# A diffusion-transformer block: two spare PSUM banks in the last attention unit, the next row's weights issued by ScalarE, and six weight pieces made earlier

## The chip, the cores and the metric

The kernel runs on one core of a Trainium2 chip. The metric is device time in microseconds (us) for one launch, lower is better. In the profile PE is TensorE (matmuls), PEld its weight loads, DVE is VectorE, ACT is ScalarE, POOL is GpSimd and SP is SyncE, which here issues most of the DMA transfers ("SPq" is its queue). "L192" is line 192 of the kernel; the matmuls go through a helper, so nearly all of them carry this line and are told apart by the names of their tiles.

## The reference

One transformer block with adaptive layer norm, in float32, for `x` of shape (2, 2048, 512) and a condition of shape (2, 512). There are 16 heads of 32 channels, the attention is causal, and the hidden layer is 2048 wide.

```python
mod = silu(condition) @ Wada + bada
sh_a, sc_a, gt_a, sh_m, sc_m, gt_m = jnp.split(mod, 6, axis=1)
xm = layernorm(x, g1, be1) * (1.0 + sc_a[:, None, :]) + sh_a[:, None, :]
q, k, v = (xm @ Wqkv)            # 16 heads of 32
attn = softmax(where(causal, q @ k.T * 32**-0.5, -inf))
x = x + gt_a[:, None, :] * ((attn @ v) @ Wproj + bproj)
xm = layernorm(x, g2, be2) * (1.0 + sc_m[:, None, :]) + sh_m[:, None, :]
x = x + gt_m[:, None, :] * (gelu(xm @ W1 + b1) @ W2 + b2)
```

## The kernel before

The two batch rows are worked one after the other, and then both go through the hidden layer. In order of time: QKV projection of row 0, attention of row 0, output projection of row 0, QKV projection of row 1, attention of row 1, output projection of row 1, hidden layer. TensorE's matmuls, and the calls wrapped in `act(...)`, are kept in the order of the program; everything else is ordered by a scheduler when the kernel is built. Each engine works its own list in order, and so does each DMA queue: an entry that waits holds up all that stand behind it.

**QKV projection** (`Qkv.run`, `Qkv.group`). Four groups `g` of 512 tokens, each with 12 products `n` (eight for queries and keys, four for values). The weights `wqkv`, 3 MB, are loaded in three pieces by `load_w`. After every product, `also(g, n)` may put in other work. In row 0 it makes the modulation out of `Wada`, whose halves pass one after the other through a tile of the pool `wada`. The `x` tiles of the next group are loaded, normalised and transposed between the products, and scores of the first attention units are put between the matmuls.

**Attention** (`attention_phase`). A unit is four heads (index `c`) and 512 queries (block `i`); there are 16, and the last has `i = 3`. A unit is worked in steps, one for each block of 128 keys: 15 steps in the last unit. In a step, `scores_t` makes the transposed scores of four heads in four PSUM banks `st`: four "fold" matmuls write the negative row maxima (`st<-fold,sel`), four more add the scores (`st<-qst,kst`), and ScalarE takes the exponential of each bank into a tile `e` (L558). Two steps later the products with the values (`o<-e,vv`) follow, and now and then the row sums (`sm<-ee,ones`). The row maxima come from scores made ahead in the two banks of the pool `ps_s` (tag `s`); in the last unit none are left to make. PSUM's eight banks are four `st` (`bufs=HC`, and HC is 4), two `s`, one `o` and one `sm`.

Each unit's sums are inverted and widened to all channels in DRAM (`wide_d`). In the last unit, `prepare(n)` readies the projection at step `n`: it loads the projection weights (`wproj`), old outputs (`at_s`) and `x` tiles into memory of keys no longer used, multiplies the weights by the gate (`ps_gate`, one matmul `ps_rows` into an `s` bank), and loads two blocks of widened inverses (`rb_s`) into old query tiles.

**Output projection** (`project_phase`). Four blocks `k` of 512 tokens in four tiles of 128. For each tile GpSimd adds the bias to the residual input (`xt`, L938), TensorE makes four products (`ps_o`), VectorE adds them to `xt` (L945), takes statistics (L204), the result goes to DRAM (`x1d`, L947), and VectorE scales one quarter of the next block's `at` by its inverses (L951). TensorE can therefore begin block `k + 1` only when VectorE has come so far with block `k`. In blocks 1 to 3 the `xt` tiles are loaded at this time, into four buffers. `between(n)` is called after each tile `n`; in row 0 it starts, at `n = 4`, the load of row 1's weights:

```python
        def between(n):
            if n == 4:
                qkv.load_w()
```

**Weight pieces** (`Quarters`). The hidden layer multiplies with a scheme of seven products in place of eight, whose weights are sums and differences of quarters. GpSimd makes them, 16 pieces in all (`FC`), each from four loads of 128 KB, five additions of 128x256 and a store of 896 KB to DRAM (`w1d`, `w2d`). All 16 are made during row 1's QKV projection; two of the four loads go to a tile of their own, `w1r`.

Of the kernel before, what the change touches and what calls it, by code (L numbers as in the profile page):

```python
# [8 lines left out]
F32 = mybir.dt.float32  # L9
# [3 lines left out]
ALU = mybir.AluOpType  # L13
# [4 lines left out]
P = 128  # L18
# [3 lines left out]
QB = 512  # L22
# [5 lines left out]
def dit_block_kernel(  # L28
# [35 lines left out]
    nc = tc.nc  # L64
    B, T, D = x.shape
    HID = W1.shape[1]
    C = D // P
    FC = HID // P
    NT = T // P
    HC = P // HD  # L70
# [3 lines left out]
    NG = T // MT  # L74
# [8 lines left out]
    def pool(name, bufs=1, **kw):  # L83
        return tc.tile_pool(name=name, bufs=bufs, reuse_waits="tile", **kw)
# [25 lines left out]
        op=ALU.add,  # L110
# [3 lines left out]
    for n in range(2):  # L114

        f = bp.tile([P, QB + P], F32R, tag=f"fold{n}", name=f"fold{n}")
# [7 lines left out]
    for r in (0, HD):  # L124
# [19 lines left out]
    bgate = bp.tile([P, D], F32, tag="bgate", name="bgate")  # L144
# [20 lines left out]
    wide_d = [  # L165
        [dram.tile([P, C, QB], F32, tag=f"wide{b}{i}", name=f"wide{b}{i}") for i in range(NQ)]
        for b in range(B)
    ]
# [25 lines left out]
    def act(ins):  # L194

        return tc.keep_in_program_order(ins)
# [14 lines left out]
    def rows_of(psum, r, b, tag):  # L211

        ps = psum.tile([P, D], F32, tag=tag, name="ps_rows")
        g = slice(r * HD, (r + 1) * HD)
        mm(ps, pick[g, b, :], modr[g, :], start=True, stop=True)
        return ps
# [43 lines left out]
    units = []  # L260
# [4 lines left out]
    last_order = [i for _, i in units[-NQ:]]  # L265
# [6 lines left out]
    ps_sp = ps_s_cm.__enter__()  # L272

    class Row:


        def __init__(self, b):
            self.b = b
            self.vv = bp.tile([P, NT, D], F32, tag="vv", name="vv")
            self.kst, self.qst, self.pools = {}, {}, {0: bp}  # L280
            self.at = 0
            self.todo = [
                (u, h, t, kb)
                for u, (_, i) in enumerate(units)
                for h in range(HC)
                for t in range(TQ)
                for kb in range(i + 1)
            ]
            self.mx = None
            self.spent = 0  # L290
            self.rows_made = 0
# [106 lines left out]
        def prepare(self, n):  # L398

            if n == 3:  # L400
                self.prefetch()
            elif n == 5:
                self.ps_gate = rows_of(ps_sp, 0, self.b, "s")
                act(nc.vector.tensor_tensor(bgate, bgate, self.ps_gate, ALU.mult))
            elif n == 7:
                self.rb_s = [self.old_queries() for _ in range(2)]
                for k in range(2):
                    nc.sync.dma_start(self.rb_s[k], wide_d[self.b][last_order[k]])
            if 5 <= n < 5 + C:
                w = self.wproj[:, n - 5, :]  # L410
                act(nc.vector.tensor_tensor(w, w, self.ps_gate, ALU.mult))
            elif 11 <= n < 11 + C:
                d, r = self.at_s[0][:, n - 11, :], self.rb_s[0][:, n - 11, :]
                act(nc.vector.tensor_tensor(d, d, r, ALU.mult))

# [97 lines left out]
    def attention_phase(row):  # L513
        b, vv, kst, qst = row.b, row.vv, row.kst, row.qst
        with pool(f"att{b}") as ap, pool(
            f"ps_st{b}", bufs=HC, space=PSUM
        ) as ps_stp, pool(f"ps_o{b}", space=PSUM) as ps_op:
            row.pools[1] = ap

            def scores_t(u, step, n):  # L520

                def st_bank():
                    return ps_stp.tile([P, QB], F32, tag="st", name="st")  # L530

                c, i = units[u]
                tiles = steps_of[u][step]
                q0 = tiles[0][1]
                w = sum(QB - q for _, q in tiles)
                sts, es = [], []
                row.score(max(0, n - 5))
                n = min(n, 5)
                for h in range(HC):
                    g = slice(h * HD, (h + 1) * HD)  # L540
                    st = st_bank()
                    mm(
                        st[:, :w], sel[g, :], fold[u % 2][g, q0 : q0 + w],
                        start=True, stop=False,
                    )
                    sts.append(st)
                for h in range(HC):
                    at = 0
                    for j, q in tiles:
                        mm(  # L550
                            sts[h][:, at : at + QB - q],
                            kst[c][:, h, j * P : (j + 1) * P],
                            qst[u][:, h, q:],
                            start=False, stop=at + QB - q == w,
                        )
                        at += QB - q
                    e = ap.tile([P, QB], F32, tag="e", name="e", bufs=E_BUFS)
                    act(nc.scalar.activation(e[:, :w], sts[h][:, :w], AF.Exp))  # L558
                    if tiles[0][0] >= i * TQ:

                        d = e.rearrange("p (t k) -> p t k", k=P)[:, 0 : TQ : TQ - 1, :]
                        d = d[:, : len(tiles), :]
                        act(
                            nc.gpsimd.affine_select(  # L564
                                d, d, pattern=[[0, len(tiles)], [1, P]],
                                compare_op=ALU.is_ge, fill=0.0,
                                base=0, channel_multiplier=-1,
                            )
                        )
                    es.append(e)  # L570
                    if h >= HC - n:
                        row.score(1, st_bank if h == 2 else None)
                row.score(n - HC)
                return es
# [55 lines left out]
            for u, (c, i) in enumerate(units):  # L630
                for n, tiles in enumerate(steps_of[u]):
                    w = sum(QB - q for _, q in tiles)
# [12 lines left out]
            for u, (c, i) in enumerate(units):  # L645
# [5 lines left out]
                for n_step, tiles in enumerate(steps_of[u]):  # L651
                    last = n_step == steps - 1
                    if n_step == 0:
# [4 lines left out]
                    n = row.count(  # L658
                        due(u, starts[u] + n_step) - QB // 2, u + AHEAD
                    )  # L660
# [70 lines left out]
    class Qkv:  # L731
# [12 lines left out]
                xts.append(xt)  # L744
            self.xts[g] = xts

        def load_w(self):
            w_v = Wqkv.rearrange("(c p) f -> p c f", p=P)
            for f in range(0, 3 * D, D):
                nc.sync.dma_start(self.w[:, :, f : f + D], w_v[:, :, f : f + D])  # L750

        def norm(self, g, j):

# [90 lines left out]
    w1_v = W1.rearrange("(c p) f -> p c f", p=P)  # L844
    w2_v = W2.rearrange("(c p) f -> p c f", p=P)

    class Quarters:


# [1 line left out]

        def __init__(self, cp):
            self.cp, self.at = cp, 0
            self.to = []

        def quarters(self, f):
# [13 lines left out]
                for k, n in ((0, f), (1, g), (0, g), (1, f))  # L872
            ]

        def step(self):

            while self.to:
                dst, w = self.to.pop()
                nc.gpsimd.dma_start(dst, w)
            f, self.at = self.at, self.at + 1  # L880
            if f >= FC:
                return
            w = self.cp.tile([P, 7, C // 2, P], F32, tag="w7", name="w7", bufs=2)
            raw = self.cp.tile([P, 2, C // 2, P], F32, tag="w1r", name="w1r", bufs=2)
            for dst, src in zip((w[:, 2], w[:, 1], raw[:, 0], raw[:, 1]), self.quarters(f)):
                nc.gpsimd.dma_start(dst, src)
            for n, x, y, op in (
                (0, w[:, 2], w[:, 1], ALU.add),
                (3, w[:, 2], raw[:, 0], ALU.add),
                (4, raw[:, 1], w[:, 1], ALU.add),  # L890
                (5, raw[:, 1], w[:, 2], ALU.subtract),
                (6, w[:, 1], raw[:, 0], ALU.subtract),
            ):
                nc.gpsimd.tensor_tensor(w[:, n], x, y, op)
            if f < FC // 2:
                self.to.append((w1d[f], w))
            else:
                self.to.append(
                    (w2d[:, f - FC // 2], w.rearrange("p n c d -> p n (c d)"))
                )  # L900
# [58 lines left out]
    with pool("wada") as wp, pool("qkv0") as qp, pool(  # L959
# [32 lines left out]
        qkv = Qkv(row, qp, ps_mm)  # L992
        qkv.load_x(0)
        load_wada(0, 1)
        qkv.load_w()

        ps_c = ps_mm.tile([P, n_rows], F32, tag="mm", name="ps_c")
        transpose(ps_c, rows)
# [46 lines left out]

        def also(g, n):

            if g == 0 and n == 2:
                load_wada(2, 5)
            elif g == 1 and n == 3:  # L1050
                modulation(2)
                load_wada(3, 4)
            elif g == 2 and n == 3:
                modulation(3)
                scale_shift(a2, c2, r_g2, r_be2, 3, 4)

        with pool("hl0") as hp:
            qkv.run(hp, also)

    attention_phase(row)  # L1060


    first, row = row, Row(1)
    with pool("qkv1") as qp, pool("ps_qkv1", bufs=6, space=PSUM) as ps_mm:
        qkv = Qkv(row, qp, ps_mm)
        qkv.xts[0] = first.next_s

        def between(n):
            if n == 4:
                qkv.load_w()  # L1070
            if n in (5, 8):
                qkv.norm(0, n // 8)()

        project_phase(first, ps_mm, between)

        def also(g, n):
            if n % 3 == 1:
                quarters.step()

        with pool("hl1") as hp:  # L1080
            quarters = Quarters(hp)
            qkv.run(hp, also)
            quarters.step()

    attention_phase(row)
    ps_s_cm.__exit__(None, None, None)
# [350 lines left out]
```

## Time and profile before

| what | value |
|---|---|
| median of 3 runs | 2528.28 us (2524.02 to 2534.17) |
| the profiled execution: its own time, its span | 2531.33 us, 2529.6 us |
| PE busy | 2464.2 us, 97% of the span |
| PEld, DVE, ACT, POOL busy | 46%, 53%, 35%, 39% |
| granted TensorE clock, mean | 0.990 |
| DMA | 285.71 MB, mean 113 GB/s |
| QKV projection of row 0 | about 21 to 223 us |
| last attention unit of row 0, of row 1 | 753.9 to 805.5, 1604.5 to 1656.2 us |
| output projection of row 0, of row 1 | 805.5 to 874.6, 1656.2 to 1718.2 us |
| QKV projection of row 1 | 874.6 to 1074 us |
| hidden layer | 1718.2 us to the end |

A line of a timeline has the start, the time it took, the engine, the line, the operation, its output and inputs with their shapes, the number of instructions that were merged, and in brackets the idle time before it and what ended that. A line of stretches has, for each engine, busy time and number of instructions, then the granted clock, the DMA engines' busy share and GB/s. A matmul's end is modelled, so a matmul that waits inside a group of merged ones is drawn longer, and not as idle time.

### The profile page before, as it was taken

The numbers are of one execution on the slowest core, as the hardware profiler recorded it, in microseconds if no ns is written. First come the engines' busy times: TensorE is split into PE (matmuls) and PEld (weight loads), VectorE is DVE, ScalarE is ACT, GpSimd is POOL, SyncE is SP. The second block draws the span as 40 slices with busy tenths as digits, with TensorE's granted clock in tenths as the row PEclk, the third lists the DMA queues.
The fourth block names the chain that finished last, engine by engine and source line by source line (L and its number), as shares of the span: only waits on it lengthen the run. The fifth ranks groups of instructions, "written<-read, shape, count | busy, mean of one in ns | idle before, by whom it ended". The sixth has DMA issues, their size and how long they took to land.

```text
span 2529.6 us, 30921 instructions
## 1 busy us (share of the span) xinstructions
PE 2464.2 (97%) x10977; PEld 1174.0 (46%) x10977; DVE 1347.6 (53%) x2818; ACT 895.0 (35%) x1667; POOL 981.4 (39%) x1158
## 2 busy tenths in 40 slices
PE   7999999999999899999999999999999999999998
PEld 3445445454444344554444444444444444444443
DVE  3455657666556535656675756565353353344424
ACT  2213555555544011155545454613312312311310
POOL 0001776766761476168667775231101201200200
PEclk9999999999999999999999999999999999999999
DMA  6636123041332699540414113163223233322422
GB/s 223 207 123 155 39 59 77 22 109 43 96 114 91 212 302 295 172 102 22 109 43 103 32 47 137 52 213 125 85 94 127 90 100 106 110 91 73 139 84 96
DMA packets 133445, 285.71 MB, mean 113 GB/s; under 512 B 13301, under 2 KB 42525, under 8 KB 128426
## 3 DMA queue, kind: packets, MB, share of 16 engines
q1 hardware_dynamic: 127810, 260.61, 34.6%
q0 software_dynamic: 5376, 23.07, 2.6%
q8 instruction: 86, 1.41, 0.2%
q14 instruction: 69, 0.57, 0.1%
q10 hardware_dynamic: 104, 0.05, 0.0%
HBM read 209.76 MB, written 81.79 MB: 115 GB/s over the span
## 4 chain that ended last, share of the span: by engine, by line
PE 60%; DVE 2%; DMA 2%; SPq 1%; issue 1%; ACT 0%; POOL 0%; DVEq 0%; ACTq 0%; POOLq 0%
PE ps_y L192 15%; PE ps_h L192 15%; PE st L192 9%; PE o L192 5%; PE s L192 4%; PE ps_qk L192 4%; PE sm L192 2%; PE ps_o L192 2%; PE ps_v L192 2%; SPq L336 1%; DMA k<-hl 1%; PE ps_xt L200 1%; DVE junk L434 1%; DMA r<-sum 1%; DVE mx L439 0%
## 5 line engine op out<-in xcount | busy, mean ns | idle before, releaser
L558 ACT ACTIVATE e<-st 128x512 f32<-128x512 f32 (+1 forms) x1152 | 575.0, 576 | 516.4 <-PE st L192 467.3
L439 DVE TENSOR_REDUCE mx<-s 128x1 f32<-128x512 f32 x616 | 413.7, 687 | 274.5 <-PE s L192 273.3
L584 POOL TENSOR_TENSOR ee<-e 128x512 f32<-128x512 f32 x336 | 421.3, 1290 | 246.0 <-ACT e L558 245.5
L192 PE MATMUL s<-kst,qst 128*128 128x512 f32 (+3 forms) x1058 | 453.3, 447 | 18.7 <-DVE mx L434 9.2
L192 PE MATMUL st<-qst,kst 128*128 128x512 f32 (+3 forms) x1280 | 437.0, 391 | 0.0
L192 PE MATMUL o<-e,vv 128*32 128x512 f32 (+3 forms) x2560 | 295.6, 543 | 0.0
L192 PE MATMUL ps_h<-sx,w 128*128 128x512 f32 x640 | 286.7, 592 | 0.0
L564 POOL TENSOR_SCALAR_AFFINE_SELECT e<-e 128x128 f32<-128x128 f32 (+1 forms) x384 | 123.6, 340 | 416.8 <-ACT e L558 410.1
L434 DVE CUSTOM_DVE_ANT_0 junk<-s,causal 128x384 bf16<-128x384 f32 (+3 forms) x442 | 211.1, 478 | 135.6 <-PE s L192 126.9
L1208 POOL TENSOR_TENSOR c<-c 128x512 f32<-128x512 f32 x32 | 40.8, 1274 | 619.9 <-DVE c L1170 619.9
L192 PE MATMUL ps_y<-sh,w 128*128 128x512 f32 x640 | 277.9, 594 | 0.0
L192 PEld LDWEIGHTS st<-qst,kst 128*128 128x128 f32 x1280 | 229.5, 191 | 87.7 <-issue 63.1
L192 PEld LDWEIGHTS s<-kst,qst 128*128 128x128 f32 x1058 | 198.8, 189 | 144.2 <-issue 47.9
L192 PE MATMUL ps_qk<-xmT,wqkv 128*128 128x512 f32 x512 | 242.0, 601 | 2.2 <-DVE xmT L248 2.2
L1170 DVE TENSOR_TENSOR h<-c,ps_h 128x512 f32<-128x512 f32 x128 | 88.0, 688 | 232.5 <-PE ps_h L192 232.4
L584 POOL TENSOR_TENSOR ee<-ee 128x512 f32<-128x512 f32 x168 | 211.0, 1286 | 0.0
L192 PEld LDWEIGHTS ps_h<-sx,w 128*128 128x128 f32 x640 | 121.1, 190 | 150.2 <-issue 149.2
L192 PEld LDWEIGHTS ps_y<-sh,w 128*128 128x128 f32 x640 | 121.3, 191 | 148.6 <-issue 147.1
L192 PE MATMUL st<-fold,sel 32*128 32x512 f32 (+1 forms) x1152 | 163.6, 484 | 2.4 <-DVE mhl L454 1.1
L1194 ACT ACTIVATE h<-h,cols 128x512 f32<-128x512 f32 x128 | 92.4, 722 | 182.0 <-DVE h L1170 182.0
L192 PEld LDWEIGHTS st<-fold,sel 32*128 32x128 f32 x1152 | 65.5, 183 | 187.8 <-ACT e L558 136.5
L192 PEld LDWEIGHTS ps_qk<-xmT,wqkv 128*128 128x128 f32 x512 | 95.4, 193 | 98.8 <-issue 91.5
(126 smaller groups left out, 2362.3 us busy)
## 6 DMA issues: line engine op xcount, KB each, us to landing
qst<-q SPq DMA_DIRECT2D x128, 256.0 KB
w<-w1d SPq DMA_DIRECT2D x34, 896.0 KB
w<-w2d SPq DMA_DIRECT2D x28, 1024.0 KB
kst<-k SPq DMA_DIRECT2D x24, 1024.0 KB
q<-hl SPq DMA_DIRECT2D x32, 512.0 KB
k<-hl SPq DMA_DIRECT2D x32, 512.0 KB
kst<-k SPq DMA_DIRECT2D x32, 256.0 KB
o<-ot SPq DMA_DIRECT2D x32, 256.0 KB
```

Source lines behind the costliest of these rows:

```text
L192: return tc.keep_in_program_order(nc.tensor.matmul(*args, **kw))
L200: return tc.keep_in_program_order(nc.tensor.transpose(dst, src, ident[:n, :n]))
L336: nc.sync.dma_start(dst, inv_d[self.b][u].unsqueeze(1).to_broadcast([HC, HD, QB]),)
L434: nc.vector.tensor_tensor_reduce(junk[:, :w], s[:, :w], causal[:, QB - w :], 1.0, MASKED, ALU.add, ALU.max, m,)
L439: nc.vector.tensor_reduce(m, s[:, :w], axis=AX.X, op=ALU.max)
L558: act(nc.scalar.activation(e[:, :w], sts[h][:, :w], AF.Exp))
L564: nc.gpsimd.affine_select(d, d, pattern=[[0, len(tiles)], [1, P]], compare_op=ALU.is_ge, fill=0.0, base=0, channel_multiplier=-1,)
L584: act(engine.tensor_tensor(dst, x, y, ALU.add))
L1170: nc.vector.tensor_tensor(dst, x, y, op)
L1194: nc.scalar.activation(d, d, AF.Gelu, bias=col(r_b1 + chunk, 1))
L1208: nc.gpsimd.tensor_tensor(c1_, c1_, c2_, ALU.subtract)
```

## The change

Four edits.

- In the last unit `st_bank` takes some of its tiles from the two `s` banks: a counter is raised for each tile, and the tile goes to `s` where the counter modulo 6 is over `HC` (4).
- `prepare` no longer holds the gate in an `s` bank for four steps: it copies it at step 5 into the first quarter of `rb_s[1]`, scales the weights from there in steps 6 to 9 (before: 5 to 8), and loads `rb_s[0]` at step 5 and `rb_s[1]` at step 10 (before: both at 7).
- `load_w` takes the queue to issue on. In row 0's output projection it is called at `n == 2` on ScalarE's queue (before: at 4, on SyncE's).
- The first six of the sixteen weight pieces are made in the last group of row 0's QKV projection, at even `n`, two at a time in the memory of the `wada` tile; the other ten in row 1's, where a step comes every fourth product in place of every third. The two extra loads of a piece go to places of the piece itself, which are overwritten by the additions; `w1r` is gone.

TensorE's list of instructions stays as it was. ScalarE's list has the three `wqkv` loads behind the last unit's copy of `sums`.

```diff
--- before.py
+++ after.py
@@ -400,16 +400,18 @@
             if n == 3:
                 self.prefetch()
             elif n == 5:
-                self.ps_gate = rows_of(ps_sp, 0, self.b, "s")
-                act(nc.vector.tensor_tensor(bgate, bgate, self.ps_gate, ALU.mult))
-            elif n == 7:
+                ps = rows_of(ps_sp, 0, self.b, "s")
                 self.rb_s = [self.old_queries() for _ in range(2)]
-                for k in range(2):
-                    nc.sync.dma_start(self.rb_s[k], wide_d[self.b][last_order[k]])
-            if 5 <= n < 5 + C:
-                w = self.wproj[:, n - 5, :]
-                act(nc.vector.tensor_tensor(w, w, self.ps_gate, ALU.mult))
-            elif 11 <= n < 11 + C:
+                self.gate = self.rb_s[1][:, 0, :]
+                act(nc.vector.tensor_copy(self.gate, ps))
+                act(nc.vector.tensor_tensor(bgate, bgate, self.gate, ALU.mult))
+                nc.sync.dma_start(self.rb_s[0], wide_d[self.b][last_order[0]])
+            if 6 <= n < 6 + C:
+                w = self.wproj[:, n - 6, :]
+                act(nc.vector.tensor_tensor(w, w, self.gate, ALU.mult))
+            if n == 10:
+                nc.sync.dma_start(self.rb_s[1], wide_d[self.b][last_order[1]])
+            if 11 <= n < 11 + C:
                 d, r = self.at_s[0][:, n - 11, :], self.rb_s[0][:, n - 11, :]
                 act(nc.vector.tensor_tensor(d, d, r, ALU.mult))
 
@@ -517,6 +519,8 @@
         ) as ps_stp, pool(f"ps_o{b}", space=PSUM) as ps_op:
             row.pools[1] = ap
 
+            n_bank = [0]
+
             def scores_t(u, step, n):
 
 
@@ -527,6 +531,10 @@
 
 
                 def st_bank():
+
+                    n_bank[0] += u == len(units) - 1
+                    if n_bank[0] % 6 > HC:
+                        return ps_sp.tile([P, QB], F32, tag="s", name="st")
                     return ps_stp.tile([P, QB], F32, tag="st", name="st")
 
                 c, i = units[u]
@@ -744,10 +752,10 @@
                 xts.append(xt)
             self.xts[g] = xts
 
-        def load_w(self):
+        def load_w(self, queue):
             w_v = Wqkv.rearrange("(c p) f -> p c f", p=P)
             for f in range(0, 3 * D, D):
-                nc.sync.dma_start(self.w[:, :, f : f + D], w_v[:, :, f : f + D])
+                queue.dma_start(self.w[:, :, f : f + D], w_v[:, :, f : f + D])
 
         def norm(self, g, j):
 
@@ -844,6 +852,8 @@
     w1_v = W1.rearrange("(c p) f -> p c f", p=P)
     w2_v = W2.rearrange("(c p) f -> p c f", p=P)
 
+    piece = 7 * C // 2 * P
+
     class Quarters:
 
 
@@ -851,8 +861,8 @@
 
 
 
-        def __init__(self, cp):
-            self.cp, self.at = cp, 0
+        def __init__(self):
+            self.rooms, self.more_rooms, self.at = [], None, 0
             self.to = []
 
         def quarters(self, f):
@@ -872,26 +882,30 @@
                 for k, n in ((0, f), (1, g), (0, g), (1, f))
             ]
 
-        def step(self):
-
+        def store(self):
             while self.to:
                 dst, w = self.to.pop()
                 nc.gpsimd.dma_start(dst, w)
+
+        def step(self):
+
+            self.store()
             f, self.at = self.at, self.at + 1
             if f >= FC:
                 return
-            w = self.cp.tile([P, 7, C // 2, P], F32, tag="w7", name="w7", bufs=2)
-            raw = self.cp.tile([P, 2, C // 2, P], F32, tag="w1r", name="w1r", bufs=2)
-            for dst, src in zip((w[:, 2], w[:, 1], raw[:, 0], raw[:, 1]), self.quarters(f)):
-                nc.gpsimd.dma_start(dst, src)
+            if not self.rooms:
+                self.rooms = self.more_rooms()
+            w = self.rooms.pop(0).rearrange("p (n c d) -> p n c d", n=7, d=P)
+            for n, src in zip((2, 1, 6, 5), self.quarters(f)):
+                nc.gpsimd.dma_start(w[:, n], src)
             for n, x, y, op in (
-                (0, w[:, 2], w[:, 1], ALU.add),
-                (3, w[:, 2], raw[:, 0], ALU.add),
-                (4, raw[:, 1], w[:, 1], ALU.add),
-                (5, raw[:, 1], w[:, 2], ALU.subtract),
-                (6, w[:, 1], raw[:, 0], ALU.subtract),
+                (0, 2, 1, ALU.add),
+                (3, 2, 6, ALU.add),
+                (4, 5, 1, ALU.add),
+                (5, 5, 2, ALU.subtract),
+                (6, 1, 6, ALU.subtract),
             ):
-                nc.gpsimd.tensor_tensor(w[:, n], x, y, op)
+                nc.gpsimd.tensor_tensor(w[:, n], w[:, x], w[:, y], op)
             if f < FC // 2:
                 self.to.append((w1d[f], w))
             else:
@@ -992,7 +1006,7 @@
         qkv = Qkv(row, qp, ps_mm)
         qkv.load_x(0)
         load_wada(0, 1)
-        qkv.load_w()
+        qkv.load_w(nc.sync)
 
         ps_c = ps_mm.tile([P, n_rows], F32, tag="mm", name="ps_c")
         transpose(ps_c, rows)
@@ -1045,6 +1059,8 @@
 
         def also(g, n):
 
+            if g == NG - 1 and n % 2 == 0:
+                quarters.step()
             if g == 0 and n == 2:
                 load_wada(2, 5)
             elif g == 1 and n == 3:
@@ -1054,8 +1070,17 @@
                 modulation(3)
                 scale_shift(a2, c2, r_g2, r_be2, 3, 4)
 
+        quarters = Quarters()
         with pool("hl0") as hp:
+
+            def rooms():
+
+                w = wp.tile([P, 2 * C * D], F32, tag="wada", name="w7")
+                return [w[:, k * piece : (k + 1) * piece] for k in range(2)]
+
+            quarters.more_rooms = rooms
             qkv.run(hp, also)
+            quarters.store()
 
     attention_phase(row)
 
@@ -1066,21 +1091,24 @@
         qkv.xts[0] = first.next_s
 
         def between(n):
-            if n == 4:
-                qkv.load_w()
+            if n == 2:
+                qkv.load_w(nc.scalar)
             if n in (5, 8):
                 qkv.norm(0, n // 8)()
 
         project_phase(first, ps_mm, between)
 
         def also(g, n):
-            if n % 3 == 1:
+            if n % 4 == 1:
                 quarters.step()
 
         with pool("hl1") as hp:
-            quarters = Quarters(hp)
+            quarters.more_rooms = lambda: [
+                hp.tile([P, piece], F32, tag="w7", name="w7", bufs=2)
+            ]
             qkv.run(hp, also)
-            quarters.step()
+            assert quarters.at >= FC
+            quarters.store()
 
     attention_phase(row)
     ps_s_cm.__exit__(None, None, None)
```

## The prediction

> **What bounds the kernel now.** I read the page's busy shares first (PE 97%), then TensorE's waits, then three stages by timeline and by short stretches. TensorE sets the end, so an edit is worth what it takes out of TensorE's gaps, its half-clock time, or the stretched matmuls that hide a wait: a matmul that waits for its bank is drawn as busy, so the last kind is not in the idle sums.
>
> First stage, the last attention unit (row 0: 753.9 to 805.5 us; row 1 the same, 1604.5 to 1656.2). TensorE's timeline, then ScalarE's:
>
> ```profile
> 780.22 0.50 PE L192 MATMUL st<-fold,sel 32*128 32x512 f32 x4
> 780.65 1.20 PE L192 MATMUL st<-qst,kst 128*128 128x512 f32 x4
> 781.77 1.07 PE L192 MATMUL o<-e,vv 128*32 128x512 f32 x8
> 782.77 1.08 PE L192 MATMUL st<-fold,sel 32*128 32x512 f32 x4
> 783.78 1.20 PE L192 MATMUL st<-qst,kst 128*128 128x512 f32 x4
> ```
>
> ```profile
> 781.24 2.06 ACT L558 ACTIVATE e<-st 128x512 f32<-128x512 f32 x4 [1.40 <-PE st L192]
> ```
>
> The four fold matmuls of a step take 0.43 us (780.22 to 780.65) when their banks are free. Those at 782.77 take 1.01: the fourth bank is read by the fourth exp until 783.30, so they lose 0.58. ScalarE has slack: 2.06 us for four exps in a step of 3.1.
>
> Second stage, row 0's output projection. TensorE, GpSimd and SyncE's queue in time order, then stretches (PE, PEld, DVE, ACT, POOL busy, clock, DMA share, GB/s):
>
> ```profile
> 842.57 5.15 PE L192 MATMUL ps_o<-kst,at 128*128 128x512 f32 x6 [7.56 <-DVE at L951]
> ...
> 838.26 5.38 POOL L938 TENSOR_TENSOR xt<-xt,bgate 128x512 f32<-128x512 f32 x4 [9.90 <-DMA xt<-in_x_dram]
> ```
>
> ```profile
> 829.11 0.33 SPq L947 DMA_DIRECT2D x1d<-xt  x1
> 829.48 1.06 SPq L750 DMA_DIRECT2D wqkv<-in_L_cond_Wqkv_dram  x2
> 830.59 2.24 SPq L937 DMA_DIRECT2D xt<-in_x_dram  x4
> ```
>
> ```profile
> 836.00:840.00 4.00, 0.00 (x0) 0.00 (x0) 0.44 (x1) 0.00 (x0) 1.74 (x2) 1.00 1.03 395
> 840.00:844.00 4.00, 1.43 (x2) 0.50 (x2) 3.97 (x9) 0.00 (x0) 3.64 (x3) 0.52 0.67 207
> 844.00:848.00 4.00, 4.00 (x10) 1.59 (x10) 3.89 (x11) 0.00 (x0) 0.00 (x0) 0.63 0.79 270
> ```
>
> The chain: SyncE stands on one `x1d` store until 829.11, then issues 2 MB of `wqkv`, and only then the next `xt`; it lands at 838.26; GpSimd adds the bias, VectorE adds the product, and behind that in VectorE's order stands the scaling of `at` that TensorE needs: 7.56 us idle, then some 6 us at about 0.6 of the clock. From 805.48 to 874.58 are 69.1 us; 64 products of 0.86 and two groups of transposes of 0.87 make 56.7. So 12.4 are lost: 7.56, a second wait of 1.65 at 861 to 863, and 3.2 of clock.
>
> Third stage, row 1's QKV projection, VectorE then TensorE:
>
> ```profile
> 930.45 0.69 DVE L204 BATCH_NORM_STATS2 stat<-x 128x6 f32<-128x512 f32 x1 [3.12 <-DMA x<-in_x_dram]
> ...
> 932.21 0.65 PE L192 MATMUL s<-kst,qst 128*128 128x384 f32 x1 [3.09 <-DVE mx L434]
> ```
>
> An `x` tile took 7.2 us to land (chain of waits) at a DMA share of 1.0, while GpSimd moves the sixteen weight pieces (875 to 1021 us). Cost 3.1, and 1.2 by slow matmuls after it (six in 3.7 us instead of 2.6).
>
> [...]
>
> **Part A, banks.** The counter is raised before the test, so only every sixth tile (the 5th, 11th, 17th...) goes to an `s` bank: not six banks in turn. I followed it through the 15 steps: in two steps of three the last fold needs the bank of the third exp of the step before, in every third step (3, 6, 9, 12) still that of the fourth. Today's waits are those of steps 3, 4, 5, 7, 9, 10, 11, 13 (0.52 to 0.59 each) and 14 (0.36); steps 6, 8 and 12 are covered by the sum matmuls (0.88) or `ps_rows`. Kept: 3 and 9. Removed: 0.52+0.59+0.57+0.52+0.58+0.58+0.36 = 3.7. The third exp ends 0.5 before the fourth, so 0.05 to 0.09 per step remains: 3.2 per row, **6.4** in two (range 5 to 7.4).
> Added: a copy of the gate out of PSUM, 0.69 of VectorE (row of `bgate`, L404) per row, beside 24 of 40 us busy; it frees the `s` bank three steps sooner. `rb_s` is loaded 20 to 30 us later than now, but before `o<-ot` on SyncE's queue (1 MB each, about 6 us, DMA share 0.12 in 768 to 808); its readers come at step 11 and in the projection. Cost nothing; were that cover gone, 2 to 3 us.
>
> **Part B, weights by ScalarE.** Three issues (0.5 us each) go behind the `sums` copy, at about 806.4, where ScalarE does nothing but a table load and a square root until 831: free. SyncE loses them, so after the last `x1d<-kst` it issues four `xt` in a row. What it gains is less than the whole stall:
> - The eight completion semaphores are shared. In the changed order SyncE's second `x1d`, the widened inverse and the second `xt` each wait for a `wqkv` piece to land. 3.1 MB now run beside 1 MB `at`, 0.75 `rb`, 1 `at`, 1 `x1d`. At the 300 to 395 GB/s of these stretches I put the third piece at 822 to 825 (estimate from those rates), so `xt` 1 at about 827 as today, and 2 to 4 at 828 to 831 instead of 838.
> - Then VectorE's order decides. From 828.4: add 0.6, statistics 0.7, scale 0.6 a tile, with two `xmT` (0.46), one `xn` and four `x` statistics (0.6) put between. Scaled chunks at 830.7, 833.5, 837.8, 840.5; TensorE wants them at 834.0, 834.9, 835.7, 836.6. Waits 2.1 and 1.8 are late next[...].
> Loss 3.9 + about 1.5 for the later boundary and clock, against 12.4: gain **7.0**. Bounds: 1 (xt no earlier, VectorE as late) to 11. Row 1's projection has no such load: nothing.
>
> **Part C, six pieces earlier.** In row 0 GpSimd is idle before attention:
>
> ```profile
> 225.77 0.29 POOL L564 TENSOR_SCALAR_AFFINE_SELECT e<-e 128x128 f32<-128x128 f32 x1 [206.26 <-ACT e L558]
> ```
>
> The pieces reuse the `wada` tile, free after the last `ps_mod` (136.7), two at a time; the next two wait until both stores landed. A batch: six load issues of 0.72, 2.1 until they land, two more issues 1.4, ten operations of 0.73, two store issues 1.1, store landing 6.5: 22.7 us. Three end at about 205. SyncE's key load at 223.06 (it takes over that memory) and GpSimd's first select at 225.8 have 18 us to spare. The 8.4 MB pass where the DMA share is 0.0 to 1.0, mean about 0.4: cost 0, at most 3.
> Row 1 then has ten pieces. They go at the rate of buffers (9.15 us each today), so until about 967 the traffic is as dense as now, though pieces 8 to 15 (second matrix, 1 KB runs) come earlier than the 512-byte ones they replace. The 4.3 of the stall goes in about half the cases: **2.2** (range -1 to 5).
>
> **Sum.** 6.4 + 7.0 + 2.2 = 15.6 from the profiled execution's 2531.3: 2515.7. That execution is 3.0 above the median of the runs (2528.28), so the forecast is **2513**.
>
> **Rivals.**
> 1. The projection stays late: `xt` lands at 830 or later, as 3 MB share the engines with it, or VectorE's order eats the gain. For it: the semaphores above; against: 395 GB/s is reached when the queues are full. B is 1: 2519.
> 2. All three clear: A 7.4, B 11, C 5: 2505. For it: the second stage has no other wait on TensorE; against: VectorE's order.
> 3. Slower: GpSimd's batches in row 0 overrun attention's start, where the selects, the sums and the key load queue behind the last pieces. It decides from 28.8 us a batch on ((223.1 - 136.7)/3); at 40 us the overrun is 34: 2547. For it: stores took up to 7.5 us of waiting in row 1; against: DMA is half idle here.
> 4. The change doesn't do what it says: one tile in six, not two, goes to the spare banks; that is in A already.
>
> **How the numbers follow.** The forecast's case 0.63 (own range 2506 to 2519, a seventh of it above 2515.6), rival 1 0.20, rival 2 0.12, rival 3 0.05. A measurement of this kernel tells 0.5% (12.6 us) from no change: below 2515.6 faster, above 2540.9 slower. Faster 0.54 + 0.12 = 0.66, same 0.09 + 0.20 = 0.29, slower 0.05. Range 2501 to 2524: it takes in rivals 1 and 2, and leaves out the third.
>
> **What would show it.** Right: fold matmuls at 0.43 to 0.5 us but for steps 3 and 9, last unit 48.4 us instead of 51.6; `wqkv` on ScalarE's queue near 803; waits for `at` of 2 us instead of 7.6, clock 1.0 there; GpSimd done before 210 in row 0 and before 970 in row 1; no wait at `mx` near 920. Wrong: `xt` landing after 830, a 7 us wait for `at` again, or row 0's attention starting late.

## The result and the profile after

The changed kernel took 2526.93 us (median of 11 runs, 2522.04 to 2533.6), against 2534.49 for the kernel before in 11 runs beside it. The ratio is 0.9977, 95% interval 0.9964 to 0.9991: 5.8 us less (2.3 to 9.1), where 15 were forecast. Its profiled execution took 2526.39 us, span 2524.7, so 4.9 of span less than before. From the starts of the copies `ot<-o` and of the first products of each stage, the 4.9 fall out like this (after minus before, us):

| stage | difference |
|---|---|
| start of row 0's QKV projection (21.16 to 22.07), and that projection | +0.9, +0.4 |
| attention of row 0 up to the last unit | +1.7 |
| last unit of row 0 | -3.3 |
| output projection of row 0 | +1.6 |
| QKV projection of row 1 | -0.5 |
| attention of row 1 up to the last unit | -2.1 |
| last unit of row 1 | -3.3 |
| the rest | -0.4 |

**Last unit.** TensorE's timeline of the changed kernel, steps 9 and 10:

```profile
783.30 1.07 PE L192 MATMUL o<-e,vv 128*32 128x512 f32 x8
784.29 1.08 PE L192 MATMUL st<-fold,sel 32*128 32x512 f32 x4
...
786.44 1.07 PE L192 MATMUL o<-e,vv 128*32 128x512 f32 x8
787.43 0.54 PE L192 MATMUL st<-fold,sel 32*128 32x512 f32 x4
```

The folds at 784.29 (step 9) still wait for their fourth bank: 1.08 us, as long as those at 782.77 of the kernel before. Those of the next step do not (0.54).

**Projection of row 0.** SyncE's queue, ScalarE's, then VectorE, GpSimd and TensorE of the changed kernel:

```profile
805.59 0.32 SPq L619 DMA_DIRECT2D o<-ot  x1
806.09 0.53 SPq L618 DMA_DIRECT2D sum<-sums  x1
812.14 0.31 SPq L930 DMA_DIRECT2D at<-o  x1
812.51 0.42 SPq L322 DMA_DIRECT2D r<-sum  x1
...
820.77 0.32 SPq L330 DMA_DIRECT2D inv<-r  x1
...
824.73 2.70 SPq L951 DMA_DIRECT2D xt<-in_x_dram  x4
```

```profile
805.65 3.08 ACTq L758 DMA_DIRECT2D wqkv<-in_L_cond_Wqkv_dram  x3
```

```profile
820.49 0.25 DVE L329 RECIPROCAL r<-r 128x16 f32<-128x16 f32 x1 [6.63 <-DMA r<-sum]
...
820.70 0.65 DVE L965 TENSOR_TENSOR kst<-kst,qst 128x512 f32<-128x512 f32 x1
```

```profile
832.14 5.39 POOL L952 TENSOR_TENSOR xt<-xt,bgate 128x512 f32<-128x512 f32 x4 [25.43 <-DMA xt<-in_x_dram]
```

```profile
821.41 1.13 PE L192 MATMUL ps_o<-kst 128*128 128x512 f32 x2 [1.35 <-DVE kst L965]
823.53 1.12 PE L192 MATMUL ps_o<-kst 128*128 128x512 f32 x2 [0.99 <-DVE kst L965]
825.97 4.56 PE L192 MATMUL ps_o<-kst 128*128 128x512 f32 x10 [1.32 <-DVE kst L965]
...
844.28 1.33 PE L192 MATMUL ps_o<-kst,at 128*128 128x512 f32 x2 [3.94 <-DVE at L965]
846.94 2.08 PE L192 MATMUL ps_o<-kst,at 128*128 128x512 f32 x2 [1.32 <-DVE at L965]
```

Where before there was one wait of 7.56 us and one of 1.65, there are now two groups: 1.35 + 0.99 + 1.32 at 821 to 826, which is new, and 3.94 + 1.32 at 844 to 847. The clock was 0.63 and 0.51 in the stretches 844 to 848 and 848 to 852. The idle time adds up to the same, 9.1 us against 9.2: what B took from the old wait, it added in the new group. From the first `ps_o` to the first `ps_qk` are 70.5 us, 68.9 before.

The first group is the key. `sum<-sums` writes the last unit's sums (8 KB), and `r<-sum` reads them back into another layout. SyncE's waits in 803 to 830, before and then after (total us, times, longest):

```profile
SPq L330 <- DVE r L329: 3.7, 1, 3.7
...
SPq L916 <- DMA sum<-sums: 1.3, 1, 1.3
```

```profile
SPq L330 <- DVE r L329: 6.9, 1, 6.9
...
SPq L930 <- DMA sum<-sums: 5.4, 1, 5.4
```

With 3 MB of weights issued by ScalarE from 805.65 on, SyncE stands 12.3 us instead of 5.0 on this chain of two 8-KB transfers. VectorE, in its fixed order, stands 6.63 us at the reciprocal, the scaling of the second block (`kst<-kst,qst`, L965) stands behind that, and TensorE behind the scaling. SyncE gets to `xt` at 824.7. In the kernel before, the reciprocal came at 814.26 without a wait, and the chain cost TensorE nothing:

```profile
814.26 0.25 DVE L329 RECIPROCAL r<-r 128x16 f32<-128x16 f32 x1
```

What the DMA queues moved in 808 to 814 in the changed kernel shows why (packets, MB, share of the engines); q10 is ScalarE's queue, q1 SyncE's:

```profile
q10 hardware_dynamic: 985, 1.97, 100.2%
q1 hardware_dynamic: 8, 0.01, 0.4%
```

The two queues did not share evenly: in these 6 us ScalarE's moved nearly everything, while SyncE waited until 812 for 8 KB that it had issued at 806.09, 0.4 us after the weights' first piece.

**Row 1's QKV projection.** VectorE, then TensorE, of the changed kernel: the stall near 930 is there again, at 2.64 instead of 3.09 us.

```profile
931.31 0.69 DVE L204 BATCH_NORM_STATS2 stat<-x 128x6 f32<-128x512 f32 x1 [3.20 <-DMA x<-in_x_dram]
```

```profile
933.08 0.44 PE L192 MATMUL s<-kst,qst 128*128 128x384 f32 x1 [2.64 <-DVE mx L436]
```

### The profile page after: what moved, and what is told of

It is laid out like the page before. It is cut to its first block, busy times and chain, and to the rows that moved or that the text cites. A ratio compares the mean times of both kernels' runs of the same rounds, so it can differ in the third digit from the quotient of the medians.

```text
span 2524.7 us, 30931 instructions
## 1 busy us (share of the span) xinstructions
PE 2460.4 (97%) x10977; PEld 1172.8 (46%) x10977; DVE 1351.5 (54%) x2820; ACT 895.1 (35%) x1667; POOL 982.0 (39%) x1158
## 4 chain that ended last, share of the span: by engine, by line
PE 61%; DVE 2%; DMA 1%; SPq 1%; issue 0%; ACT 0%; POOL 0%; DVEq 0%; ACTq 0%
PE ps_y L192 15%; PE ps_h L192 15%; PE st L192 9%; PE o L192 5%; PE s L192 4%; PE ps_qk L192 4%; PE ps_o L192 2%; PE sm L192 2%; PE ps_v L192 2%; SPq L336 1%; PE ps_xt L200 1%; DVE junk L436 1%; PE ps_o L200 0%; DVE mx L441 0%; DMA r<-sum 0%
## 5 line engine op out<-in xcount | busy, mean ns | idle before, releaser
L192 PE MATMUL st<-fold,sel 32*128 32x512 f32 (+1 forms) x1152 | 156.8, 485 | 2.7 <-DVE fold L500 2.0
```

The costliest lines, as they stand in the source:

```text
L192: return tc.keep_in_program_order(nc.tensor.matmul(*args, **kw))
```

## The experiments

Theory: A gives what was forecast, B loses, because its weights delay the small transfers that VectorE's order hangs on, and C gives little. All in one table. "Last unit" is row 0's, from one `ot<-o` to the next; "projection" is row 0's, first `ps_o` to first `ps_qk`; "QKV 1" runs from there to the first `ot<-o`. The three times are of one trace each.

| kernel | ratio to before (95%) | last unit | projection | QKV 1 |
|---|---|---|---|---|
| before | | 44.8 | 68.9 | 219.9 |
| changed | 0.9977 (0.9964 to 0.9991) | 41.5 | 70.5 | 219.4 |
| e_banks | 0.9965 (0.9952 to 0.9977) | 41.5 | 67.2 | 222.4 |
| e_weights | 0.9998 (0.9990 to 1.0007) | 44.8 | 71.6 | 220.3 |
| e_pieces | 0.9984 (0.9976 to 0.9992) | 44.8 | 67.6 | 217.3 |
| e_nob | 0.9961 (0.9947 to 0.9976) | 41.5 | 66.8 | 221.7 |
| t_sums | 0.9947 (0.9934 to 0.9961) | 41.5 | 67.3 | 217.9 |
| t_w7 | 0.9951 (0.9934 to 0.9968) | 41.5 | 63.5 | 220.1 |
| e_dose | 0.9948 (0.9931 to 0.9965) | 41.5 | 65.2 | 219.6 |
| t_early | 0.9927 (0.9901 to 0.9952) | 41.5 | 66.9 | 214.8 |
| t_even | 0.9956 (0.9941 to 0.9971) | 40.4 | 70.2 | 219.7 |
| t_defer | 0.9959 (0.9942 to 0.9975) | 41.5 | 68.8 | 216.2 |
| t_best | 0.9934 (0.9920 to 0.9949) | 40.4 | 64.8 | 214.0 |
| t_best_early | 0.9908 (0.9893 to 0.9923) | 40.4 | 59.8 | 215.8 |

### One part alone, and part B undone

`e_banks` is the kernel before with A's lines of the diff only, `e_weights` with B's (the argument of `load_w`, step 2, `nc.scalar`), `e_pieces` with C's. `e_nob` is the changed kernel with

```diff
-            if n == 2:
-                qkv.load_w(nc.scalar)
+            if n == 4:
+                qkv.load_w(nc.sync)
```

> Part A alone on the kernel before (bank counter and the copied gate; weights on SyncE's queue and pieces as before). Theory: all of what was gained in the end comes from here: last unit 48.3 us instead of 51.6 in each row, 6.6 us in all, ratio 0.9974; the projection of row 0 with its 7.5 us wait as before (69 us from its start to the first ps_qk). Rival: the bank part also has a price in the projection (the rb_s loads that came later), then under 5 us are left and the projection is over 70 us.

> Part B alone on the kernel before. Theory: the wqkv pieces, issued from 806 us on, hold up the small r<-sum load and the o<-ot store ahead of it; VectorE stands at the reciprocal some 6 us, TensorE waits for at: projection of row 0 70 to 71 us, no gain (ratio 0.9995 to 1.001). Rival: it is the combination with part A (SyncE's rb loads moved later) that spoils it; alone it would gain the 7 us that were forecast: projection 62 us, ratio 0.997.

> Part C alone on the kernel before. Theory: QKV of row 1 gains about 0.3 us, since the remaining ten pieces still run as densely until the stall near 925 to 932, which stays at 2.5 to 3 us at mx; QKV of row 0 pays 0.3; ratio 0.9995 to 1.0005. Rival (the forecast): the stall is gone in this one and 2 us or more are gained.

> The changed kernel with part B undone (wqkv on SyncE's queue at the projection's step 4), so A and C together. Theory: B took back some of what A and C brought, so this one is faster than the changed kernel: projection of row 0 67 to 69 us from its first ps_o to the first ps_qk, with one wait of 6 to 7.6 us, ratio to the kernel before 0.995 to 0.9965. Rival: B was neutral and the changed kernel's loss is chance; ratio 0.9975.

A alone brings 8.9 us by the runs (5.8 to 12.2), more than the whole change; its last unit is the changed kernel's (41.51 and 41.49 us), and its projection pays no price for the `rb_s` loads that come later. B alone brings nothing, with the same picture as in the changed kernel: VectorE stands 6.08 us at the reciprocal, TensorE waits 0.80 + 1.00 + 1.31 and then 3.38 + 2.52. So it is B itself, not B together with A. With B undone, the ratio is 0.9961, some 4 us better than the changed kernel's, and the projection has the one wait of before (6.27 us). The two intervals overlap; the stage itself is plainer. With B as it is (changed, `e_weights`, `t_even`, `t_defer`) the projection takes 68.8 to 71.6 us, mean 70.3; without it (before, `e_banks`, `e_pieces`, `e_nob`) 66.8 to 68.9, mean 67.6. B costs some 2.7 us. VectorE's wait at the reciprocal separates them without overlap: it is 5.8 to 6.8 us in the five traces with all of B and the chain in its place (those four and `t_early`), 3.3 in `e_dose`, and at most 0.3 in the eight others.

C alone brought 4.0 us by the runs (2.0 to 6.1), against the theory that it brings nothing; its trace has 0.68 + 2.18 us of waits at `mx` where before has 3.09. More on it below.

### What in B costs

`t_sums` leaves B and moves the chain of the last sums behind; `t_w7` puts the weights behind it in SyncE's queue; `e_dose` leaves one of three pieces with ScalarE; `t_early` leaves B and takes `xt` ahead of the chain. The edits in short:

```diff
 t_sums (project_phase):
-   n == 0: row.load_sums(...)   n == 1: row.invert(...)   n == 2: row.widen(...)
+   n == 4: row.load_sums(...)   n == 6: row.invert(...)   n == 7: row.widen(...)
 t_w7 (between):
-   if n == 2: qkv.load_w(nc.scalar)
+   if n == 7: qkv.load_w(nc.sync)
 e_dose (between):
-   if n == 2: qkv.load_w(nc.scalar)
+   if n == 2: qkv.load_w(nc.scalar, 0, D)
+   if n == 7: qkv.load_w(nc.sync, D)
 t_early (project_phase, ahead of the loop over k):
+   early = [a tile xt, loaded by nc.sync, for each of the four tiles of k == 1]
```

> The changed kernel, with the last unit's chain of sums (load, reciprocal, widen) put at the projection's steps 4, 6 and 7 instead of 0, 1 and 2, so that xt and the stores go ahead of it on SyncE's queue and the reciprocal comes after the first scalings of at on VectorE. Theory (the small load r<-sum, late behind 3 MB of weights, holds VectorE and with it SyncE): the 6.6 us at RECIPROCAL r are gone, and with them the 3.7 us of TensorE at ps_o<-at and the half clock after; projection 64 to 66 us instead of 70.5, ratio to the kernel before 0.9955. Rival (the transfers themselves are late, whatever the order): xt still lands at 832, projection 70 us as in the changed kernel, ratio 0.9975.

> The changed kernel with wqkv given to SyncE at the projection's step 7 instead of ScalarE at step 2: all four xt, the sums' chain and the first stores stand ahead of it in the one queue. Theory (what is issued first takes the DMA engines; the weights need to come only at the end of the stage): r<-sum lands in 5 us as in the kernel before, no 6.6 us at RECIPROCAL r, xt land by 827, no wait of TensorE over 2.5 us, projection 61 to 64 us, ratio 0.9935 to 0.995. Rival (VectorE's order sets the time, whatever lands when): the waits for at stay at 4 us or more and the stage at 67 us, ratio 0.9965.

> The changed kernel with only the first wqkv piece (1 MB) issued by ScalarE at step 2, the other two by SyncE at step 7. Theory (the weights' bytes ahead of them are what delays the o<-ot store, r<-sum and with it VectorE): a third of the bytes, about a third of the delay: VectorE stands 1 to 3 us at RECIPROCAL r instead of 6.6, the three waits of TensorE behind it (3.7 us) shrink to under 1.5, projection of row 0 64 to 66.5 us. Rival (it is the second issuing engine that delays SyncE's transfers, whatever it carries): 5 to 7 us at the reciprocal and 69 to 71 us as in the changed kernel.

> The changed kernel, part B as it is, with the four xt of the projection's second quarter issued ahead of at and of the sums' chain. Theory (two separate waits: the first, 3.7 us at ps_o<-kst, comes of r<-sum behind the weights; the second, 5.3 us at ps_o<-kst,at with the half clock, of xt issued only at 824.7 us behind that chain): the first stays at 3 us or more, VectorE's wait at RECIPROCAL r stays at 6 us or more, the second is gone; projection of row 0 64 to 66.5 us instead of 70.5, ratio 0.995. Rival (the weights' three megabytes delay xt just as much when it is issued at 807 us): both waits stay, 69 us or more.

`t_sums`: the wait at the reciprocal and the 3.7 us behind it are gone, as the theory says, and the rival's `xt` at 832 did not come (VectorE adds the first at 828.6). But the stage took 67.3 us, not 64 to 66: SyncE now issues `xt` between stores that it waits for (819.2, then 822.1 to 823.8), and later waits came, the longest 3.17 us at 838.7.

`t_w7`: the weights are the same 3 MB, asked for later. SyncE's waits on the chain are 1.2 and 3.4 us, as before, and the reciprocal comes at 814.74 without a wait. TensorE's waits in the stage, then SyncE's queue:

```profile
837.83 1.12 PE L192 MATMUL ps_o<-kst,at 128*128 128x512 f32 x2 [1.28 <-DVE at L965]
839.95 1.12 PE L192 MATMUL ps_o<-kst,at 128*128 128x512 f32 x2 [1.00 <-DVE at L965]
...
855.70 1.13 PE L192 MATMUL ps_o<-kst,at 128*128 128x512 f32 x2 [1.73 <-DVE at L965]
858.41 11.43 PE L192 MATMUL ps_o<-kst,at 128*128 128x512 f32 x26 [1.59 <-DVE at L965]
```

```profile
821.36 1.89 SPq L951 DMA_DIRECT2D xt<-in_x_dram  x4
823.81 0.38 SPq L758 DMA_DIRECT2D wqkv<-in_L_cond_Wqkv_dram  x1
```

No wait is over 1.73 us, the matmuls between and behind the waits keep the pace of the stage's start (28 in 12.18 us from 841.79 on and 26 in 11.43 from 858.41, after 48 in 20.93), and the stage takes 63.5 us: 7.0 less than in the changed kernel. `xt` reached GpSimd at 828.8, a little later than the 827 expected, and the ratio is just over 0.995. Against the kernel before (68.9) that is 5.4 of the 7.0 us that were forecast for B, had by issuing the weights *after* `xt` and the chain. The rival, that VectorE's order alone sets the time, falls.

`e_dose` separates bytes from queue. SyncE's waits and VectorE's reciprocal:

```profile
SPq L930 <- DMA sum<-sums: 4.8, 1, 4.8
SPq L330 <- DVE r L329: 4.0, 1, 4.0
```

```profile
818.36 0.25 DVE L329 RECIPROCAL r<-r 128x16 f32<-128x16 f32 x1 [3.29 <-DMA r<-sum]
```

On the chain of two SyncE stands 4.6 us with no weights ahead (`t_w7`), 8.8 with one megabyte and 12.3 with three. One megabyte delays the first transfer nearly as much as three do (4.8 against 5.4), the second hardly (4.0 against 3.4 and 6.9): by this, what counts is what is under way when the small one is issued. VectorE stood 3.29 us, a little over the 1 to 3 expected, TensorE 1.7 instead of 1.5, the stage took 65.2. The rival, a second issuing engine that delays whatever it carries, would have given the full 5 to 7 us.

`t_early`: the first group of waits stays (3.11 + 1.31 us, 5.82 at the reciprocal), the second shrinks from 5.3 to 1.66. So they are two waits with two causes: the chain, and the late `xt`. The stage took 66.9 us, over the 64 to 66.5; after the 3.11 us the clock was at 0.54 and 0.61 in 824 to 832. Its ratio, 0.9927, owes only part to this edit: its trace is 11.5 us shorter than the changed kernel's, but the projection only 3.6, and 4.7 lie in row 1's QKV projection, which varies from trace to trace (below).

### Parts A and C carried further

The edits in short:

```diff
 t_even (st_bank):
-   if n_bank[0] % 6 > HC:
+   if n_bank[0] % 6 >= HC:
 t_defer (also, row 1):
+   at (g, n) == (1, 5): nc.gpsimd.tensor_copy(the first room's column 0, mv1 of the third group's last tile)
-   if n % 4 == 1: quarters.step()
+   if (g, n) >= (1, 5) and n % 3 == 2: quarters.step()
```

> The changed kernel with the counter's test at >= HC, so that two tiles of six go to the spare banks (six banks in turn). Theory (the bank of the exp still running is the only thing that the folds wait for): the 1.08 us folds of steps 3 and 9 become 0.43 to 0.6, last unit 47.0 to 47.4 us instead of 48.3, 2 to 2.5 us in two rows, ratio 0.9968. Rival (ps_rows, copied out of an s bank in step 5, and the sums now collide with them): no gain, or a wait at ps_rows.

> The changed kernel with row 1's ten weight pieces held back: the first waits, by a one-column copy, for the statistics of the last x tile of the third group (about 932 us), so that no piece moves while the x tiles of the second and third groups land; they then end near 1030. Theory (the x tile that lands 7 us late does so because GpSimd's pieces fill the DMA engines): the stall of 2.6 us at mx near 930 and the slow matmuls after it are gone, row 1's QKV 216.5 to 217.5 us (first ps_qk to the first ot) instead of 219.4, ratio 0.9968. Rival (x, q and k traffic alone does it): the stall stays, 219 us.

`t_even`: the folds of steps 1 to 13 take 0.50 or 0.51 us, in steps 3 and 9 as well (those of step 14 take 0.39), and the last unit 40.45 us instead of 41.49, in both rows. The wait at `ps_rows` that the rival named is there too, 0.5 us once in each row (none in the changed kernel), and is within the 40.45. The theory holds; the gain is 2.1 us in the two rows, of the 2 to 2.5 expected.

`t_defer`: the stage went from 219.4 to 216.2 us, the waits at `mx` to 0.83 and 1.09. But the copy did not hold the pieces back until 932. The loads and four of the additions of the first piece ran at 875 to 882, since they do not touch the copied column; the other nine pieces began after the copy, at 914.88, still ahead of the issue of three `x` tiles (two at 916.8, one at 920.7). In the three traces with this edit (`t_defer`, `t_best`, `t_best_early`) the stage took 214.0 to 216.2 us, mean 215.3, against 214.8 to 221.7, mean 218.8, in the eight with ten pieces started at once. Shown is only that starting nine of the ten some 40 us later shortens the stage; that it is their traffic at the moment of the `x` loads is not.

### Together

`t_best` is `t_even`, `t_w7` and `t_defer` in one; `t_best_early` adds `t_early`.

> All that gained alone, put together on the changed kernel: two spare-bank tiles of six, wqkv by SyncE at step 7, row 1's pieces held back. Theory (they lie in three stages and don't touch each other): last units 47.3 us, projection 63 to 64 us, row 1's QKV 216 to 217 us; 2.1 + 6.8 + 3 us less than the changed kernel, ratio to the kernel before 0.9925 to 0.994. Rival (what one stage saves, the next waits for, as transfers of row 1's first x tiles and keys come no earlier): ratio 0.995 or more.

> As t_best, with the four xt of the projection's second quarter issued ahead of at and of the sums' chain (they wait for nothing). Theory (xt is what GpSimd, then VectorE, then TensorE wait for at the quarter's end): no VectorE wait for xt near 830, and the waits of 1.3 and 1.0 us of TensorE at 838 to 841 are gone: projection 61 to 62 us, 2 us less than t_best, ratio 0.992. Rival (the megabyte of xt ahead of at delays at and the sums' chain by 3 us, so the waits only move to the scalings before): 63 us or more, ratio as t_best or higher.

`t_best` is within what was expected by its ratio; its projection took 64.8 us, over the 63 to 64, as waits of 2.44 and 1.59 us were followed by slow matmuls (26 in 14.28 us, 11.43 in `t_w7`). `t_best_early` is the fastest: 2512.45 us beside 2533.1 before, 23.3 us less by the ratio (19.5 to 27.1), and ahead of the changed kernel too. What is left of TensorE's waits in its projection is one line of the list of waits:

```profile
PE ps_o L192 <- DVE at L972: 2.3, 2, 1.6
```

The stage took 59.8 us, less than expected: the 56.7 of the prediction's count of the work, 2.3 of waits, and 0.8.

## Why the prediction was wrong

The number 2513 stood on 2528.28 us for the kernel before, a median of three runs; in eleven runs it is 2534.49. So 6.2 of the 13.9 us between forecast and measurement come from the base. The remaining 7.7 are the change itself: it brought 5.8 us by the ratio (7.6 between the medians), where 15 were forecast.

**A was right**, mechanism and size: 6.6 us in the two last units (3.3 + 3.3) for 6.4. Steps 3 and 9 kept their wait as worked out; the folds of the others took 0.39 to 0.59, so the "0.05 to 0.09 per step" were there too. The gate's copy and the later `rb_s` loads cost nothing that a trace shows.

**B is the step that failed**: forecast 7.0, measured -1.6 in the pair of traces and about -2.7 in four against four, outside its bounds of 1 to 11. The failing sentence is the one that sums the bytes: it put "3.1 MB now run beside 1 MB `at`, 0.75 `rb`, 1 `at`, 1 `x1d`", computed when the *large* pieces land, and from there only asked when `xt` comes. That sum was nearly right: the third piece landed at 820.7 us, forecast at 822 to 825. But the two 8-KB transfers in the same list of issues were put at nothing, though the prediction itself adds up the bytes of both issuers. They stood on the path three times: SyncE waited for the first before it went on to `at` and `xt`, VectorE for the second ahead of its scaling, TensorE for the scaling. The semaphores that were to hold up SyncE do not show: its list of waits has no `wqkv`, and all three pieces had landed before the instructions that were named. (In `e_weights` the list puts one wait of 4.8 us, at `at<-o`, down to a `wqkv` piece. The wait ended at 815.50; `sum<-sums` had landed at 815.48, the last part of that piece only at 815.68.) `xt` reached GpSimd at 832.1, not 827, and the second group of waits came to 5.3 us, not 3.9, and the clock behind the longer one was 0.63 and 0.51, where boundary and clock together were put at about 1.5 us. That ScalarE has the time for the issues was right (3.08 us that nobody waits for).

The first rival had the right symptoms (`xt` after 830, the gain eaten by VectorE's order), but it still put B at a gain of 1 us, and it did not name the two small transfers either.

**C** went about as put in sum, not in detail. GpSimd was done at 194 us in row 0, sooner than the 205 worked out (the stores that start a batch are 19.2 us apart, not 22.7), and at 969 in row 1, as forecast. The stall near 930, which was to go in half the cases, was gone in one (`t_early`, 0.36 us left) of eight traces with ten pieces started at once, and varied in the others; in these eight the stage took 214.8 to 221.7 us, mean 218.8, against 219.9, 220.3 and 222.4 (mean 220.9) with sixteen. That is 2.1 us on average, and a single trace cannot tell it. Row 0's QKV projection, put at 0, took 0.7 more on average (224.5 in eleven traces with C, 223.8 in three without). Of this 0.4 fall into its first 40 products, which end 97 us before the first piece is begun; so at most 0.3 is left for C. The runs of `e_pieces` say 4.0 (2.0 to 6.1). Between 1 and 4 the size stays open, and so does the cause.

**What chance added.** In the changed kernel's trace one unit of row 0's attention took 2.5 us longer than before (33.84 and 31.37). Other kernels with the same code up to there do not have it (31.38 in `t_early`): see the last section.

## What to carry to other kernels

When a large load is moved earlier or to a free queue, list every small transfer that is issued after it until it has landed, and ask which engine's fixed order hangs on each; the megabytes' own landing time is the lesser question. In these runs the bytes that were issued first went first, by ScalarE (1.97 of 1.98 MB in 808 to 814 of the changed kernel) as by SyncE (`t_w7`, 4.6 us on the chain in place of 12.3): what is needed last should be asked for last, and loads that wait for nothing (here `xt`) are worth issuing ahead of chains that do (`t_best_early`). One such order is left untried: even in the kernel before, `r<-sum` is issued 0.4 us behind 1 MB of `at<-o` (808.37, 808.73), and 5.5 us pass until the reciprocal can use it. A counter's test decides how many banks really take turns: following it through the steps gave A to a few tenths.

## What the runs showed of the hardware

**Small transfers under load.** From the issue of `sum<-sums` (8 KB) to SyncE's next issue, which waits for it, were 2.0 us before (806.36 to 808.37) and 6.05 after (806.09 to 812.14), with the engines at a share of 0.99 in 808 to 812. With no weights ahead of it, the small store took 2.0 us; issued just behind them, three times as long.

**The clock after short waits.** Stretches of the same work in the changed kernel and then in `e_banks` (PE, PEld, DVE, ACT, POOL busy, clock, DMA share, GB/s):

```profile
448.00:452.00 4.00, 3.77 (x19) 2.12 (x12) 2.24 (x10) 0.60 (x1) 1.61 (x2) 0.64 0.00 2
452.00:456.00 4.00, 4.00 (x18) 2.19 (x16) 2.56 (x10) 1.79 (x3) 2.71 (x5) 0.51 0.01 4
```

```profile
448.00:452.00 4.00, 3.78 (x24) 2.11 (x25) 3.23 (x11) 0.85 (x2) 2.40 (x3) 1.00 0.00 0
452.00:456.00 4.00, 3.71 (x25) 2.03 (x24) 2.78 (x14) 2.10 (x6) 3.73 (x6) 1.00 0.01 4
```

Ahead of both stand the same three waits of TensorE, 0.67, 0.38 and 0.23 us in one and 0.64, 0.38 and 0.22 in the other, within 3.3 us. In the changed kernel the clock then fell to 0.64 and 0.51 in these stretches, and the unit took 33.84 us (435.40 to 469.24); in `e_banks` it stayed at 1.00. The kernel before has the three waits too (0.65, 0.38 and 0.22 us, 444.5 to 447.7), then a clock of 1.00 and 31.37 us for the unit. `t_early`, whose code is the changed kernel's up to there, took 31.38. The slow unit came in 6 of the 14 traces, in 8 it did not.

Nor does a longer wait always bring it: behind the single wait of 1.65 us in the kernel before's projection (861.5 to 863.2) the clock was 1.00 in 860 to 868. What decides between the two was not shown; no run was made for it.

A difference of 2.5 us in one stage of one trace is therefore no evidence on this kernel.
